# Sorted expert tiles, search steps and the end: a new division of TensorE's order in an attention and expert block

## The chip, the core and the metric

One core of a Trainium2 chip runs the whole program. The metric is the device time of one execution in microseconds (us), as the median of many; one more execution was profiled. The engines are PE (TensorE, matmuls; its weight loads are a row of their own, PEld), DVE (VectorE), ACT (ScalarE), POOL (GpSimd) and SP (SyncE, whose queue issues most DMAs). Each works through its own queue in order, and they wait for each other by semaphores.

## The reference

One block of a transformer with modulation from a condition vector, over x of 4 batches x 2048 tokens x 256 channels, all in float32:

```
mod = silu(c) @ wmod                     # six vectors per batch: sa, ca, ga, sb, cb, gb
h = layernorm(x) * (1 + ca) + sa
x = x + ga * attention(h)                # 8 heads of 32, causal softmax, a rank-one term per head
h = layernorm(x) * (1 + cb) + sb
x = x + gb * experts(h)

def experts(h):                          # h: 8192 rows of 256
    shared = sum over 2 experts of gelu(h @ up) @ down
    probs = softmax(h @ router.T)        # 16 routed experts
    top 4 of probs -> gate               # each row goes to four experts
    routed = sum over these of (gelu(h @ up_e) * gate_e) @ down_e
    return shared + routed
```

## The kernel before

The 8192 rows are cut into 16 blocks of 512; a batch has four. Block i has qb = i % 4, and its attention sees the qb + 1 blocks of its batch so far. Each block has a *search*: the largest score of every row and head is found first (`max_steps`), so that the exponentials later need no second pass. One search step (`scores`) makes the scores of 4 heads for 128 rows against up to 512 keys: 8 matmuls on PE into `ps`, then two reduces on DVE into `parts` (two more adds where the causal edge lies). Block i has 8 (qb + 1) steps. The tiles `ps` come from `mring`, three buffers of which a step needs two.

The *sums* (`sum_steps`) make the scores again, transposed (`st`), subtract the maxima by a matmul with `mT`, take exponentials on ACT (`p`), and add up values (`av`) and denominators (`dv`). Where DVE has room, two neighbouring `p` are added first (a *join*), which saves one group of `dv` matmuls.

The main loop goes over the blocks. Each turn has two parts:

- the *first part* of block i: everything that PE has to do between the sums of block i - 1 and those of block i. This is the output projection of block i - 1 (`po`), the turn and the shared expert of block i - 2 (`ptb`, `pl`, `pu_-2`, `pd_s`), projections of a coming block (`pta`, `ppq`, `ppk`, `pv`), sorted expert tiles (`px`, `pu`, `py`), and search steps of block i + 1;
- the *second part*: the sums of block i, with the search steps that are left (`rest`) put between them, and DVE's and POOL's work for other blocks (`put`).

Blocks 0 to 13 send their rows to the routed experts by sorting: in five groups (blocks 0-1, then three blocks each) the rows are scattered to DRAM by expert (`xg`, one POOL DMA for 128 rows), worked off in groups of four tiles of 128 rows (`tile_steps`: `turn` = `px`, `up` = `pu`, `down` = `py`), and gathered back with their weights (`combine_steps`: `got`, then `sum` on DVE). The first load of a group's rows (`xr`) waits for all its scatters. `fetch_ahead` issues row and weight loads two groups ahead on SP. Blocks 14 and 15 run all 16 experts densely after the loop, in pairs (`dense_steps`: `ups`, `weigh`, `routed`), with expert weights held in the keys' buffer (`resident`). This is the *end*.

The order of PE's instructions is fixed in the program by a planner with guessed costs (`T_US`, `X_US`, ..., `M_US` = 1.2 for a step on PE, `M_VE` = 2.7 on DVE). For a first part, `take_tiles` decides how many sorted tiles it gets; a loop picks m, the number of search steps; `fill_in` lays out both. It issues a step when its clock t has reached the guessed end of DVE's last step, then adds `M_US` to t and DVE's cost to that; else it takes the next piece of PE's work. When less than 3 us of pieces are left, all steps that remain come out at once. `merged` mixes two lists by their shares. `tick`, called at a pace, issues one scatter or gather.

The lines of the choice in the loop:

```
now = take_tiles(1e9 if last else max(whole - own, backlog - 105.0))
filler = own + sum(us for us, _ in now)
m, busy = 0, begin
while m < len(tops) and (
    busy + tops[m][0] <= filler + 2.0 or len(tops) - m > int(0.9 * ks)
):
```

`own` is the guessed PE time of the pieces without tiles and steps, `whole` DVE's guessed time for all steps, `backlog` that of the tiles waiting, `tops` the steps, and ks the number of summing steps of the second part.

Of the kernel before, what the change touches and what calls it, by code (L numbers as in the profile page):

```python
# [12 lines left out]
F32 = mybir.dt.float32  # L13
# [6 lines left out]
P = 128  # L20
# [74 lines left out]
def adaln_block_kernel(  # L95
# [405 lines left out]
    def tick(add=True):  # L501
        for due in sums_due:
            due[0] -= 1
        if add and sums_due and sums_due[0][0] <= 0:
            sums_due[0][1].pop(0)()
            if not sums_due[0][1]:
                sums_due.pop(0)
        if scatters:
            scatters.pop(0)()
            return  # L510
        if not gathers and ready and len(sums_due) < 2:
            gathers.extend(ready[0][0])
        if gathers:
            gathers.pop(0)()
            if not gathers:
                sums_due.append([3, ready.pop(0)[1]])


    def fill_in(pieces, tops=(), begin=0.0, pace=3.2, add=False):

        pieces, tops = list(pieces), list(tops)
        t, free, turns, next_tick = 0.0, begin, [], 1.0
        while pieces or tops:
            if t >= next_tick:
                tick(add)
                next_tick = t + pace
            if tops and (t >= free - 0.3 or sum(us for us, _ in pieces) < 3.0):
                ve, steps, turn = tops.pop(0)  # L530
                t = max(t, free)
                for s in steps:
                    s()
                t += M_US
                free = t + ve
                if turn is not None:
                    turns.append([3, turn])
                continue
# [583 lines left out]

    chain = {"steps": [], "turned": 0, "done": 0, "rows": 0, "weights": 0}

    def fetch_ahead():
        for what, n, done in (("rows", 0, "turned"), ("weights", 1, "done")):
            while chain[what] < min(len(chain["steps"]), chain[done] + 2):
                step = chain["steps"][chain[what]]  # L1130
                chain[what] += 1
                step[n](step[2])

    def tile_steps(group):
# [82 lines left out]
        for q in range(count):  # L1217
            pieces.append((U_US, lambda q=q: up(q)))
            if q + 1 < count:
                pieces += [(X_US, lambda q=q, h=h: turn(q + 1, h)) for h in range(2)]  # L1220
            pieces += [(D_US, lambda q=q, h=h: down(q, h)) for h in range(2)]
        return pieces

    def combine_steps(group):
# [56 lines left out]
    def dense_steps(i):  # L1281
# [17 lines left out]
                )  # L1299

        def up(e, u):
            if u == 0:
                acts[e] = probs.tile([P, 2, QB], F32, tag="pt", name=f"act{i}_{e}")
            pu = single([P, QB], f"pu{i}_{e}_{u}")
            products(pu, e, u)
            nc.scalar.activation(acts[e][:, u, :], pu, AF.Gelu)
# [103 lines left out]

    def take_tiles(us):
        got = []
        while tiles_to_come and us > 0:
            got.append(tiles_to_come.pop(0))
            us -= got[-1][0]
        return got

    def tiles_of(group):
        pieces = tile_steps(group)
        us, last = pieces[-1]  # L1420

        def end():
            last()
            ready.extend(combine_steps(group))

        tiles_to_come.extend(pieces[:-1] + [(us, end)])

    def free(steps):
# [4 lines left out]
    for i in range(NBLK):  # L1433
# [4 lines left out]
        if i:  # L1438
            soon, later = projected_in(i)
            outs = out_steps(i - 1, oT)  # L1440
            turns, ups, downs = [], [], []
            if i > 1:
                turns = turn_steps(i - 2)
                ups, downs = dense_steps(i - 2)
            begin = 2.5
            lead, mid = [], []
            if soon:
                new = project_steps(soon[0])
                lead = new[:2] + turns[:2] + new[2:6]
# [12 lines left out]
            mid = mid[:at] + tail  # L1462

            for n, s in enumerate(ends):
                (lead or mid).insert(2 * n + 1, (0.001, s))
            tops = [] if last else maxima(i + 1)
            state["pairs"] = not last
            own = sum(us for us, _ in lead + mid)
            whole = begin + sum(ve for ve, _, _ in tops)
            backlog = sum(us for us, _ in tiles_to_come)  # L1470
            now = take_tiles(1e9 if last else max(whole - own, backlog - 105.0))
            filler = own + sum(us for us, _ in now)
            m, busy = 0, begin
            while m < len(tops) and (
                busy + tops[m][0] <= filler + 2.0 or len(tops) - m > int(0.9 * ks)
            ):
                busy += tops[m][0]
                m += 1
            rest = tops[m:]
            left = fill_in(lead + (merged(mid, now) if now and mid else mid), tops[:m], begin)  # L1480
        if filled is not None and not scatters:
            tiles_of(filled)
            filled = None
# [103 lines left out]


    state["summing"] = True
    for e in range(0, R, 4):  # L1590
        nc.sync.dma_start(
            out=resident[:, e * 2 * C : (e + 4) * 2 * C].rearrange("p (e n) -> p e n", e=4),
# [18 lines left out]
        begin.insert(n + 1, (0.001, s))  # L1611
    begin += outs[:1] + choice[:2] + outs[1:] + ups
    begin += choice[2:-1] + downs[:1] + choice[-1:] + downs[1:]
    fill_in(begin + in_turn(pairs[:1]), pace=1.3, add=True)
    while scatters:
        tick()
    tiles_of(filled)
    choice = free(choice_steps(j, None))
    norms = second_norm_steps(j)
    late = turn_steps(j) + choice[:1] + more + choice[1:]  # L1620
    rest = take_tiles(1e9)
    amid = in_turn(pairs[1:6])
# [48 lines left out]
```

## Time and profile before

| | |
|---|---|
| median of 17 runs | 2482.15 us (2469.57 to 2492.84) |
| the profiled execution | 2475.79 us |
| its span | 2474.1 us, 42120 instructions |
| mean granted PE clock | 0.961 |
| main loop before the first sorted tile | 0 to 522.8 us |
| main loop after it (first part of block 4 to second part of block 15) | 522.8 to 2204.6 us |
| end | 2204.6 to 2474.1 us |

The parts are told apart in the timeline: a second part lasts from a block's first `st` to its last `av` or `dv`. All of the program's instructions go through one helper, so nearly all have its line (L54); they are known by the tiles they write. A timeline row has its start, its length, engine, line, operation, tiles out<-in, shapes, the number of instructions merged, and in brackets the idle time of the engine before it and what ended it. A row of busy time by stretch has the stretch, its length, then for each engine the busy time and the number of instructions, the granted clock of PE, and DMA's share and GB/s. A busy PE includes matmuls at half clock.

### The profile page before, as it was taken

The numbers are of one execution on the slowest core, as the hardware profiler recorded it, in microseconds if no ns is written. First come the engines' busy times: TensorE is split into PE (matmuls) and PEld (weight loads), VectorE is DVE, ScalarE is ACT, GpSimd is POOL, SyncE is SP. The second block draws the span as 40 slices with busy tenths as digits, with TensorE's granted clock in tenths as the row PEclk, the third lists the DMA queues.
The fourth block names the chain that finished last, engine by engine and source line by source line (L and its number), as shares of the span: only waits on it lengthen the run. The fifth ranks groups of instructions, "written<-read, shape, count | busy, mean of one in ns | idle before, by whom it ended". The sixth has DMA issues, their size and how long they took to land.

```text
span 2474.1 us, 42120 instructions
## 1 busy us (share of the span) xinstructions
PE 2328.7 (94%) x16625; PEld 1157.8 (47%) x16625; DVE 1435.3 (58%) x2789; ACT 980.3 (40%) x1391; POOL 733.5 (30%) x740
## 2 busy tenths in 40 slices
PE   7999999999999999999999998998999999998987
PEld 4443434345554334355545435354545635345754
DVE  5676565536665765646675656847665665642335
ACT  2323234543334334533343344643344345543420
POOL 3201010331101244601013352611344035464324
PEclk9889899999999899999999899999999989998998
DMA  3200401343430212322534225222656734347943
GB/s 122 90 1 10 153 10 65 126 151 112 160 120 10 70 62 97 113 93 93 188 105 154 84 63 196 79 89 88 227 175 212 247 118 157 117 147 270 341 137 112
DMA packets 219702, 306.88 MB, mean 124 GB/s; under 512 B 18544, under 2 KB 158832, under 8 KB 219504
## 3 DMA queue, kind: packets, MB, share of 16 engines
q1 hardware_dynamic: 192720, 228.89, 27.8%
q0 software_dynamic: 25536, 73.43, 9.2%
q8 instruction: 131, 2.15, 0.4%
q10 hardware_dynamic: 1248, 1.86, 0.2%
q14 instruction: 67, 0.55, 0.1%
HBM read 193.49 MB, written 114.82 MB: 125 GB/s over the span
## 4 chain that ended last, share of the span: by engine, by line
PE 83%; DVE 7%; ACT 3%; DMA 3%; issue 2%; POOL 1%; SPq 0%; POOLq 0%; ACTq 0%; DVEq 0%
PE st L54 18%; PE ps L54 13%; PE av L54 11%; PE dv L54 8%; PE pu L54 8%; PE py L54 5%; DVE parts L54 4%; PE pv L54 3%; PE po L54 2%; PE ppq L54 2%; PE px L54 2%; PE ppk L54 2%; PE pd L54 2%; PE pd_s L54 2%; PE pl L54 1%
## 5 line engine op out<-in xcount | busy, mean ns | idle before, releaser
L54 DVE TENSOR_REDUCE parts<-ps 128x2 f32<-128x1024 f32 (+3 forms) x640 | 662.4, 1063 | 366.9 <-PE ps L54 358.0
L54 ACT ACTIVATE p<-st 128x1024 f32<-128x1024 f32 (+3 forms) x640 | 539.0, 893 | 512.2 <-PE st L54 454.1
L54 PE MATMUL st<-qT,kv 32*128 32x512 f32 (+3 forms) x2560 | 406.6, 586 | 13.8 <-ACT p L54 7.4
L54 PE MATMUL ps<-kv,qT 32*128 32x512 f32 (+3 forms) x2560 | 388.4, 609 | 17.2 <-DVE parts L54 11.6
L54 POOL DMA_INDIRECT got<-yg,at x224 | 231.6, 1034 | 338.8 <-ACT p L54 102.2
L54 PE MATMUL av<-p,kv 128*32 128x512 f32 (+3 forms) x2560 | 303.4, 546 | 0.0
L74 POOL DMA_INDIRECT xg<-rows,at x219 | 219.4, 1002 | 263.0 <-ACT p L54 92.2
L54 PEld LDWEIGHTS st<-qT,kv 32*128 32x128 f32 x2560 | 144.7, 186 | 265.9 <-issue 148.4
L54 PE MATMUL dv<-p,ones 128*32 128x512 f32 (+3 forms) x2224 | 251.8, 527 | 2.7 <-DVE p L54 2.7
L54 DVE TENSOR_TENSOR ps<-ps,cmask 128x256 f32<-128x256 f32 x256 | 109.2, 427 | 200.7 <-PE ps L54 173.2
L54 PEld LDWEIGHTS ps<-kv,qT 32*128 32x128 f32 x2560 | 126.6, 192 | 205.5 <-issue 103.2
L54 POOL TENSOR_TENSOR x<-x,tmps 128x512 f32<-128x512 f32 x28 | 35.4, 1264 | 503.6 <-DVE tmps L54 503.4
L54 PE MATMUL py<-wt,tact 128*128 128x256 f32 x608 | 164.4, 406 | 6.9 <-ACT xt L54 4.8
L54 PE MATMUL st<-mT,unit 3*128 3x512 bf16 (+3 forms) x1280 | 166.7, 349 | 0.0
L54 PEld LDWEIGHTS pu<-xt,wt 128*128 128x128 f32 x1216 | 146.1, 194 | 36.4 <-issue 18.6
L54 PE MATMUL pu<-xt,wt 128*128 128x128 f32 x1216 | 157.1, 282 | 2.7 <-DMA wt<-experts 1.4
L54 ACT COPY y<-py 128x512 f32<-128x512 f32 x152 | 89.0, 585 | 166.1 <-PE py L54 166.0
L54 PEld LDWEIGHTS py<-wt,tact 128*128 128x128 f32 x608 | 112.1, 198 | 61.8 <-issue 12.9
L54 ACT COPY xt<-px 128x512 f32<-128x512 f32 x152 | 85.1, 587 | 111.1 <-PE px L54 111.1
L54 PEld LDWEIGHTS dv<-p,ones 128*32 128x32 f32 x2224 | 63.0, 110 | 138.1 <-issue 121.2
L54 DVE TENSOR_TENSOR p<-p,p 128x1024 f32<-128x1024 f32 x84 | 107.1, 1315 | 33.8 <-PE av L54 33.5
L54 ACT ACTIVATE tact<-pu 128x512 f32<-128x512 f32 x76 | 45.4, 597 | 190.5 <-PE pu L54 190.5
(290 smaller groups left out, 2476.2 us busy)
## 6 DMA issues: line engine op xcount, KB each, us to landing
wt<-experts SPq DMA_DIRECT2D x304, 256.0 KB, 4.2
xr<-xg SPq DMA_DIRECT2D x76, 512.0 KB, 4.8
yg<-y SPq DMA_DIRECT2D x76, 512.0 KB, 3.3
xg<-zeros SPq DMA_DIRECT2D x16, 1024.0 KB, 9.5
xin<-in_x SPq DMA_DIRECT2D x16, 512.0 KB, 5.7
x<-in_x SPq DMA_DIRECT2D x16, 512.0 KB, 4.5
h2d<-xnb POOLq DMA_DIRECT2D x14, 512.0 KB
pre<-x POOLq DMA_DIRECT2D x14, 512.0 KB
```

The source lines that it names most:

```text
L54: made = call(*args, **kwargs)
L74: made = call()
```

## The change

Eight edits, all in the planner, in the order of what PE, POOL and SP get; what is computed is unchanged.

1. `tick`: a gather goes ahead of waiting scatters when a set of gathers is begun, or when fewer than five sets are ready.
2. `fill_in`: the next tick comes 2.2 us later while scatters or gathers wait, otherwise after `pace`.
3. `take_tiles`: a group's second `py` is never split from what comes ahead of it.
4. Tiles for a first part: as many as fill the guessed idle time, in which a search step's PE time now counts; the backlog that may stay is 80 us instead of 105.
5. m: a step's PE time counts as cover for DVE (`+ M_US * m - 5.0`), and after a block with qb = 0 all steps go to the first part.
6. The first three pieces (one, for the last block) come ahead of any tile (`ahead`).
7. The shared activation of block 15 lies in oT's buffer.
8. The end: the last group's tiles are announced before the resident weights are loaded, with its row loads held until all scatters are out (`held`, `release`); two pairs instead of one come ahead of the tiles; block 15's turn and choice stand further ahead; the last stretch has pace 0.4 instead of 1.6.

```diff
-        if scatters:
+
+        if scatters and not (gathers or 0 < len(ready) < 5 and len(sums_due) < 2):
             scatters.pop(0)()
             return
...
             if t >= next_tick:
+                next_tick = t + (2.2 if scatters or ready else pace)
                 tick(add)
-                next_tick = t + pace
...
         for what, n, done in (("rows", 0, "turned"), ("weights", 1, "done")):
+            if what == "rows" and chain["held"]:
+                continue
...
             pieces += [(D_US, lambda q=q, h=h: down(q, h)) for h in range(2)]
+            pieces[-1][1].follows = True
...
-            if u == 0:
+            if u == 0 and i + 1 == NBLK:
+                acts[e] = once.tile([P, 2, QB], F32, tag="oT", name=f"act{i}_{e}")
+            elif u == 0:
                 acts[e] = probs.tile([P, 2, QB], F32, tag="pt", name=f"act{i}_{e}")
...
-        while tiles_to_come and us > 0:
+
+        while tiles_to_come and (us > 0 or hasattr(tiles_to_come[0][1], "follows")):
...
-            now = take_tiles(1e9 if last else max(whole - own, backlog - 105.0))
+
+
+            idle = whole - own - M_US * len(tops)
+            now = take_tiles(1e9 if last else max(idle, backlog - 80.0))
             filler = own + sum(us for us, _ in now)
             m, busy = 0, begin
+            most = 0 if qb == 0 else int(0.9 * ks)
             while m < len(tops) and (
-                busy + tops[m][0] <= filler + 2.0 or len(tops) - m > int(0.9 * ks)
+                busy + tops[m][0] <= filler + M_US * m - 5.0 or len(tops) - m > most
             ):
...
-            left = fill_in(lead + (merged(mid, now) if now and mid else mid), tops[:m], begin)
+
+            if now:
+                ahead = 1 if last else 3
+                mid = mid[:ahead] + merged(mid[ahead:], now)
+            left = fill_in(lead + mid, tops[:m], begin)
...
+    chain["held"] = True
+    tiles_of(filled)
...
-    fill_in(begin + in_turn(pairs[:1]), pace=1.3, add=True)
-    while scatters:
-        tick()
-    tiles_of(filled)
+
+    def release():
+        while scatters:
+            tick()
+        chain["held"] = False
+        fetch_ahead()
+
+    first = in_turn(pairs[:2])
+    fill_in(begin + first[:3] + [(0.001, release)] + first[3:], pace=1.3, add=True)
+    assert not scatters
     choice = free(choice_steps(j, None))
     norms = second_norm_steps(j)
-    late = turn_steps(j) + choice[:1] + more + choice[1:]
+    late = turn_steps(j) + choice[:1] + more[:1] + choice[1:3] + more[1:] + choice[3:4]
     rest = take_tiles(1e9)
-    amid = in_turn(pairs[1:6])
-    fill_in(free(norms) + merged(rest[:30], amid[:9]) + merged(rest[30:], amid[9:] + late), pace=2.4, add=True)
-    fill_in(in_turn(pairs[6:]) + much + in_turn(others), pace=1.6, add=True)
+    amid = in_turn(pairs[2:6])
+    for n, step in enumerate(choice[4:6]):
+        amid.insert(9 + 2 * n, step)
+    amid = amid[:7] + late + amid[7:]
+    fill_in(free(norms) + merged(rest, amid) + choice[6:], pace=2.4, add=True)
+    fill_in(in_turn(pairs[6:]) + much + in_turn(others), pace=0.4, add=True)
```

What the built programs' PE queues hold by part, before > after. A part of block i has search steps of block i + 1; "at its end, alone" counts the steps of a first part between which and behind which no other work stands but a projection, an output or a short turn. Parts not listed, and everything ahead of block 4, are the same.

| block | steps in first part | of these at its end, alone | steps in second part | four-tile groups (`pu`) in first part |
|---|---|---|---|---|
| 4 | 16 | 3 > 8 | 0 | 4 > 1 |
| 5 | 24 > 21 | 3 > 9 | 0 > 3 | 7 > 3 |
| 6 | 11 > 30 | 3 > 12 | 21 > 2 | 1 > 5 |
| 7 | 3 > 6 | none | 5 > 2 | 0 > 1 |
| 8 | 16 | 3 > none | 0 | 4 > 6 |
| 9 | 24 > 21 | 3 > 9 | 0 > 3 | 7 > 3 |
| 10 | 19 > 30 | 3 > 12 | 13 > 2 | 5 |
| 11 | 8 | none | 0 | 3 > 8 |
| 12 | 16 | 2 > 8 | 0 | 4 > 0 |
| 13 | 24 > 21 | 3 > 9 | 0 > 3 | 7 > 3 |
| 14 | 32 | 5 > 6 | 0 | 13 |
| 15 | 0 | none | 0 | 5 > 12 |

All `dv` matmuls together are 28 fewer after (each is two instructions of PE); no other kind changes in number.

More of the change, by code (lines that the diff above doesn't have):

```diff
@@ L1121, in place_steps @@
         return steps + [(1.4, 0, lambda: past(0)), (1.4, 0, lambda: past(1)), (0.2, 0, owners)]
-    chain = {"steps": [], "turned": 0, "done": 0, "rows": 0, "weights": 0}
+    chain = {"steps": [], "turned": 0, "done": 0, "rows": 0, "weights": 0, "held": False}
     def fetch_ahead():
         for what, n, done in (("rows", 0, "turned"), ("weights", 1, "done")):
+            if what == "rows" and chain["held"]:
+                continue
             while chain[what] < min(len(chain["steps"]), chain[done] + 2):
@@ L1424, in end @@
             ready.extend(combine_steps(group))
+        end.follows = True
         tiles_to_come.extend(pieces[:-1] + [(us, end)])
```

## The prediction, made before the changed kernel ran

> **What bounds the kernel now.** I read the page's busy times first, then busy time by stretch with the bounds of the blocks' two parts, then the timeline where TensorE (PE) and its clock lose time.
>
> ```profile
> PE 2328.7 (94%) x16625; PEld 1157.8 (47%) x16625; DVE 1435.3 (58%) x2789; ACT 980.3 (40%) x1391; POOL 733.5 (30%) x740
> PE 83%; DVE 7%; ACT 3%; DMA 3%; issue 2%; POOL 1%; SPq 0%; POOLq 0%; ACTq 0%; DVEq 0%
> 817.80:936.30 118.50, 113.77 (x894) 35.88 (x894) 81.31 (x160) 44.92 (x56) 38.44 (x41) 0.92 0.17 55
> 952.90:1058.00 105.10, 103.27 (x943) 34.11 (x942) 57.60 (x137) 60.18 (x71) 57.23 (x54) 1.00 0.36 119
> 1385.40:1482.60 97.20, 95.80 (x825) 31.90 (x825) 47.63 (x98) 44.17 (x54) 38.70 (x42) 0.94 0.23 73
> 1998.40:2071.90 73.50, 69.89 (x671) 23.41 (x670) 50.89 (x110) 44.21 (x55) 42.20 (x40) 0.98 0.39 120
> 2111.00:2204.60 93.60, 92.73 (x873) 30.52 (x873) 53.67 (x113) 59.65 (x71) 55.16 (x52) 1.00 0.29 92
> ```
>
> PE sets the end, and its total work hardly changes. A reordering can win only PE's waits and half-clock time. The stretches are the second parts of blocks 6, 7, 10, 14 and 15 (columns: length, busy PE, weight load, DVE, ACT, POOL, then granted clock, DMA share, GB/s). Blocks 6, 10 and 14 sum the same scores, yet 6, with 21 search steps inside, takes 118.5 us; 10, with 13, 97.2; 14, with none, 73.5.
>
> ```profile
> 153.40:169.60 16.20, 14.75 (x56) 5.49 (x56) 14.75 (x17) 0.72 0.00 0
> 159.34 10.30 PE L54 MATMUL ps<-kv,qT 32*128 32x512 f32 x32 [0.43 <-DVE parts L54]
> 160.72 5.37 DVE L54 TENSOR_REDUCE parts<-ps 128x2 f32<-128x512 f32 x5
> 169.57 3.78 PE L54 MATMUL po<-wo,oT 128*128 128x256 f32 x8
> 716.75 1.99 PE L54 MATMUL ps<-kv,qT 32*128 32x512 f32 x12
> 722.52 1.13 PE L54 MATMUL py<-wt,tact 128*128 128x256 f32 x4
> 1981.95:1994.30 12.35, 11.63 (x42) 4.28 (x41) 12.25 (x14) 0.58 (x1) 0.00 (x0) 0.69 0.04 14
> ```
>
> (The first row, of the search's instructions alone, lists PE, weight load and DVE, then the clock.) These are stretches in which PE's queue holds nothing but search steps ("runs"). In the first part of block 1, seven steps last from 153.49 to 169.57: 2.30 us each, set by DVE, whose two reduces take 1.2 us each. Five in block 14's take 12.35 (2.47 each); three in block 5's 5.77. One step alone costs PE some 1.0 us at full clock (1.14 busy, 1.07 to the next start). The two long runs also halve the clock (0.72, 0.69).
>
> ```profile
> 1490.48 1.09 PE L54 MATMUL px<-ident,xr 128*128 128x128 f32 x4 [7.57 <-DMA xr<-xg]
> 1729.05 6.06 POOL L54 TENSOR_TENSOR xnb<-xnb,gm 128x256 f32<-128x256 f32 x8 [13.49 <-PE py L54]
> 1735.17 0.48 PE L54 MATMUL ptb<-ident,xnb 128*128 128x128 f32 x1 [1.00 <-POOL xnb L54]
> 2244.56 1.94 PE L54 MATMUL px<-ident,xr 128*128 128x128 f32 x8 [7.83 <-DMA xr<-xg]
> 2374.87 0.62 PE L54 MATMUL pgt<-ident_b,gate 128*48 128x128 bf16 x4 [6.24 <-DVE gate L54]
> ```
>
> The largest plain waits: sorted rows that come after their scatters (block 11, and the end), the normed rows of POOL (block 13), a late gate (the end).
>
> **The change part by part.** Everything before 522.8 us stays in its order.
>
> *Runs.* The new bound on m counts a step's 1.2 us as cover for DVE, while `fill_in` still spaces steps by 1.2 us plus DVE's own 2.7. So pieces run out before steps do. In the changed order the runs at the ends of first parts 4, 5, 6, 9, 10, 12, 13, 14 are 8, 9, 12, 9, 12, 8, 9, 6 steps: 73. Before they were 3, 3, 3, 3, 3, 2, 3, 5, and 3 in block 8, which loses its run. Beyond its own 1.0 us a step of a long run costs 1.30 to 1.47; I take 1.38. After: 73 x 1.38 = 100.7. Before, seven of three steps, one of two (3.5 us by the timeline) and one of five: 7 x (5.8 - 3) + (3.5 - 2) + (12.35 - 5) = 28.4. Loss 72 (67 to 79). Behind a run stand the last projections and the next block's st on PE's queue, and ACT's exponentials wait for these.
>
> *Clock behind the runs.* After the run at 153 us the next po takes 3.78 us where the one before it took 2.00, and the first st 1.57 where the next takes 1.23: 2.1 us. After the short runs of blocks 4, 5, 9, 12, 13 the clock stays 1.00; these five now get a drop, block 8 loses one: 4 x 2.1 = 8 (0 to 11).
>
> The Trainium skill, "TensorE: Matmul & The Clock Gate", section "HAM oscillation", says PE keeps its clock unless it idles for over about 3.4 us. In the run at 153 us no idle exceeds 0.47 us, yet the clock is halved; I go by the row. By the page these 8 us would be 0.
>
> *Rows of POOL (`ahead = 3`).* In first parts 5, 9, 13 the first ptb now follows two pta; before, tile pieces came ahead of it. The xnb it needs is finished 8.3, 8.2 and 15.2 us after the second part ends (632.9 - 624.6, 1168.0 - 1159.8, 1735.1 - 1719.9). PE then has 1.1 us of work to put there (1.6 in block 13), so loses 7.2, 7.1, 13.6. Before, it lost 5.7, 6.1, 10.1 (10.8, 11.2, 15.7 us to the ptb, less 5.1, 5.1, 5.6 of work). That is 6, and half clock after the wait in blocks 5 and 9, 2 x 2.1: 10 (0 to 16). Behind that ptb waits all of the first part, so DVE's search starts later too; DVE has the slack for it there.
>
> *Second parts.* Steps leave blocks 6 (21 to 2), 10 (13 to 2), 7 (5 to 2); three each enter 5, 9, 13. A step in block 6 costs (118.5 - 73.5 - 6 dv groups at 0.95) / 21 = 1.87, 0.87 beyond its own 1.0; in block 10 0.38; in block 7 (against block 15, three dv groups, narrower steps of 0.75) 0.98. So 19 x 0.87 + 11 x 0.38 + 3 x 0.98 = 23.6, less 9 x 0.6: -18 (-4 to -20, by block 10's price or block 6's). 28 dv matmuls fewer are seven groups of 0.95: -7. Their joins (two adds of 1.3 us) fall into DVE's idle time; without that cover each would delay the dv behind it.
>
> *Scatters, gathers.* In `tick` gathers pass scatters only when few are ready. Of the 48 scatters of blocks 5 to 7, 44 now stand before block 10's second part (28 before), so block 11's row loads no longer come late: 7.6 us and 2.4 of the half clock behind it, -10 (0 to -10). The 32 gathers that leave blocks 6 and 7 for 8 and 9 cost POOL 1.03 us each, issued where it is 30% busy; block 10's first part gets 40 scatters, at 1.27 us from start to start 51 us of about a hundred.
>
> *End.* A second pair of dense experts (8.2 us) now covers the scatters, but on SP's queue the four loads of resident weights now stand ahead of the last rows load, and POOL has 18 scatters left instead of 16: -5.5 (0 to -8). The gate is chosen earlier: 6.2 and 1.7 of clock, -8. PE ends 15 us before the span; with a gather per piece (pace 0.4), 50 fit into the last ten pairs, of 48 needed: -7 (0 to -11). The sorted tiles lie denser where DMA's share is already 1.03: +2 (0 to 8). Together -18.5.
>
> At nothing: the eight expert loads that move ahead of the resident weights on SP's queue go out beside block 15's second part (DMA share 0.29); without that they would hold the rows back 4.5 us, their issue time at 2242. The last block's activation in oT's place finds oT read by po long before; else it would wait for the two po, 4 us.
>
> **Sum.** 72 + 8 + 10 - 18 - 7 - 10 - 18.5 = +36.5. The profiled execution took 2475.8 us (span 2474.1), so 2512 for it; it lies 6.4 below the median of 2482.15, so the median comes to 2519. With the terms' bounds taken as independent (15 down, 27 up), the forecast's own range is 2504 to 2546.
>
> **Rivals.**
>
> *Runs are cheap (not slower).* Place: the eight runs. The three-step runs cost 0.93 beyond their own time, since PE is a step and a half ahead of DVE when a run begins, and keep the clock. If long ones did too, runs would cost 73 x 0.93 - 28.4 = 39.5 and the clock nothing: 40.5 less, -4: 2478; without the 10 for POOL's rows 2468. It decides from 0.98 us a step downwards. For it: five short runs. Against it: two long ones at 1.30 and 1.47, and PE's lead is used up after two steps.
>
> *The end gives nothing (slower still).* If the denser tiles wait for DMA (share 1.03 at 2275 to 2300 us) and the last rows come later behind the resident weights, the 20.5 us of the end go and 6 come: 2545. For it: the saturated stretch. Against: at that share PE waited only 0.54 us for weights.
>
> *The change does not do what it says.* It speaks of keeping tiles for long searches, yet first parts 4, 5, 9, 12, 13 lose three to five groups of four sorted tiles each by the order; 6, 8, 11 and 15 gain. That speaks for the forecast.
>
> **How the numbers follow.** Forecast 0.62, cheap runs 0.22, no gain at the end 0.16. The cheap-run case lies about no change: 0.17 faster by over 0.2% (what this measurement can tell), 0.05 within it. The rest is slower: 0.78. The range goes from inside the first rival to the second: 2472 to 2548.
>
> **What would show it.** Runs of eight to twelve ps steps at the ends of the named first parts, over 2.2 us a step, with a clock near 0.7; a ptb wait of 6 us or more early in first parts 5, 9, 13; the second part of block 6 near 80 us, of block 10 near 78; no px wait in block 11; the pgt wait gone. Wrong: runs under 2 us a step, or second parts shorter than block 14's.

## The result, and the profile after

The changed kernel takes 2571.42 us (median of 8 runs, 2568.15 to 2576.84), against 2481.8 for the kernel before in the same hours (46 runs): a ratio of 1.0366, 95% interval 1.035 to 1.0382. That is some 90 us slower. The forecast was slower by 36.5, and the time lies outside its range. The profiled execution took 2568.5 us, with a span of 2566.8 (2474.1 before) and a mean granted clock of 0.937 (0.961 before).

The changed kernel's page, busy times and the chain that ended last by engine:

```profile
PE 2371.0 (92%) x16569; PEld 1187.0 (46%) x16569; DVE 1456.1 (57%) x2803; ACT 979.2 (38%) x1391; POOL 731.3 (28%) x740
PE 77%; DVE 7%; DMA 5%; issue 4%; ACT 3%; POOL 3%; SPq 0%; POOLq 0%; ACTq 0%; DVEq 0%
```

PE has 56 instructions less, as the order said, and is busy 42 us longer: nearly the same work, more of it at a lower clock. The share of the chain that is not PE's grew from 17% to 23%, with DMA, issue and POOL taking it. The loss is thus of two kinds, slower PE work and more waiting.

Busy time by stretch, changed kernel, the second parts of blocks 6, 10 and 14 (columns as in the table of before):

```profile
862.60:937.80 75.20, 74.33 (x708) 25.14 (x707) 33.98 (x85) 44.76 (x56) 25.10 (x27) 1.00 0.13 43
1423.90:1502.70 78.80, 76.54 (x699) 25.79 (x698) 29.91 (x64) 44.74 (x55) 11.67 (x14) 0.95 0.04 14
2033.40:2103.30 69.90, 69.30 (x676) 23.70 (x675) 53.02 (x119) 44.49 (x55) 42.63 (x41) 1.00 0.31 94
```

Block 6's fell from 118.5 to 75.2 us and block 10's from 97.2 to 78.8, as forecast (80 and 78). The search steps that left them went to the first parts. There, by stretch again, are block 6's first part, and within it the run of twelve steps at its end:

```profile
758.60:862.60 104.00, 97.40 (x508) 55.60 (x508) 76.62 (x94) 23.65 (x41) 5.81 (x5) 0.87 0.36 117
832.70:859.60 26.90, 25.15 (x98) 10.76 (x97) 25.95 (x30) 0.60 (x1) 0.00 (x0) 0.60 0.25 80
```

In the run DVE is busy 25.95 of 26.9 us, PE moves at DVE's pace, 2.24 us a step, and its clock is 0.60. The timeline of the changed kernel's PE shows the waits:

```profile
1774.43 0.48 PE L54 MATMUL ptb<-ident,xnb 128*128 128x128 f32 x1 [8.09 <-POOL xnb L54]
...
2109.73 1.12 PE L54 MATMUL ptb<-ident,xnb 128*128 128x128 f32 x4 [4.04 <-DVE rd L54]
...
2328.41 1.94 PE L54 MATMUL px<-ident,xr 128*128 128x128 f32 x8 [12.88 <-DMA xr<-xg]
```

The first is block 13's wait for POOL's rows, which was expected. In blocks 5 and 9, where waits of over 6 us were expected too, the first `ptb` waits only four times 1.0 to 1.4 us, 4.3 and 5.0 in all. The second row, in block 15, was not expected. The third is the end's wait for the last sorted rows: 7.83 us before, 12.88 now, where 2.3 were expected. SP's timeline, of the four loads of resident weights (`kv`) and of the last load of rows for the scatters:

```profile
2282.19 2.80 SPq L54 DMA_DIRECT2D kv<-experts  x4
2297.30 0.37 SPq L54 DMA_DIRECT2D rows<-h2d  x1
```

The rows of block 13 are loaded 13.3 us after the end began (at 2284.0); before it was 5.6. The end as a whole, by stretch up to the first `px`, then up to PE's last matmul, then the tail, first in the kernel before:

```profile
2204.60:2244.60 40.00, 27.28 (x95) 18.23 (x96) 16.88 (x46) 5.92 (x10) 25.93 (x29) 0.81 0.57 207
2244.60:2458.80 214.20, 204.29 (x954) 145.10 (x954) 75.29 (x161) 66.04 (x104) 79.54 (x84) 0.97 0.69 228
2458.80:2474.10 15.30, 0.00 (x0) 0.00 (x0) 9.51 (x20) 0.00 (x0) 6.30 (x6) 0.58 0.49 146
```

and in the changed kernel:

```profile
2284.00:2328.40 44.40, 30.20 (x120) 19.16 (x121) 15.73 (x46) 6.92 (x11) 28.07 (x29) 0.90 0.57 201
2328.40:2531.90 203.50, 197.10 (x928) 140.52 (x928) 64.60 (x132) 64.78 (x103) 64.61 (x69) 0.99 0.64 213
2531.90:2566.80 34.90, 0.00 (x0) 0.00 (x0) 19.40 (x44) 0.00 (x0) 19.89 (x20) 0.54 0.48 143
```

The middle is 10.7 us shorter: a pair of dense experts (7.6 us) moved ahead of it, and the wait for the late gate (6.2 us) went, while PE's waits for expert weights grew by 2.2. The stretch up to the first `px` took in that pair and 5.1 us more of waiting and is only 4.4 us longer: its other waits shrank and its clock rose from 0.81 to 0.90, some 8 us that the forecast didn't have. But the program goes on for 34.9 us after PE's last matmul, where it was 15.3. In that tail POOL issues 20 gathers (6 before). The changed kernel's POOL timeline shows why they are left:

```profile
2503.63 0.94 POOL L54 DMA_INDIRECT got<-yg,at  x1 [5.42 <-ACT act L54]
2504.88 0.95 POOL L54 DMA_INDIRECT got<-yg,at  x1 [0.30 <-issue]
2506.13 1.14 POOL L54 DMA_INDIRECT got<-yg,at  x1 [0.30 <-issue]
2511.25 0.95 POOL L54 DMA_INDIRECT got<-yg,at  x1 [3.98 <-ACT act L54]
2512.50 0.95 POOL L54 DMA_INDIRECT got<-yg,at  x1 [0.30 <-DVE act L54]
2518.87 0.94 POOL L54 DMA_INDIRECT got<-yg,at  x1 [5.42 <-ACT act L54]
```

Each gather takes 1.25 us from start to start. POOL gets three, then two for each pair of dense experts (7.6 us) and idles 4 to 5.4 us between. It isn't short of time: the program gives it too few gathers. The cause stands in the diff. Edit 8 asks for a pace of 0.4 us, but edit 2 replaces any pace by 2.2 us while sets of gathers are waiting, and they always are.

### The same by the terms of the forecast

For each part I worked out PE's time at full clock from the durations of its kinds of instructions (a group of four tiles 4.89 us, a full search step 1.07, a set of `dv` 0.95) and took it from the part's length. What is left is its loss. The changes of the loss, so work that only moved drops out:

| term | forecast | measured |
|---|---|---|
| first parts with runs, and block 8's, which loses its run (runs 72, clock 8, POOL's rows 10) | +90 | +82 |
| second parts (-18) and fewer `dv` (-7) | -25 | -17 |
| block 11's first part (`px` wait) | -10 | -1 |
| first parts of blocks 7 and 15 | 0 | +14 |
| everything ahead of block 4 | 0 | +2 |
| end | -18.5 | +13 |
| sum | +36.5 | +93 |

The run steps alone took 167.7 us for 73 steps (58.3 for 28 before, three of those in block 8), a loss beyond 1.0 us a step of 94.7 against 30.3: +64 of the forecast's 72.

### The profile page after: what moved, and what is told of

Its sections match the earlier page's. It is cut to its first block, busy times and chain, and to the rows that moved or that the text cites. A ratio compares the mean times of both kernels' runs of the same rounds, so it can differ in the third digit from the quotient of the medians.

```text
span 2566.8 us, 42060 instructions
## 1 busy us (share of the span) xinstructions
PE 2371.0 (92%) x16569; PEld 1187.0 (46%) x16569; DVE 1456.1 (57%) x2803; ACT 979.2 (38%) x1391; POOL 731.3 (28%) x740
## 3 DMA queue, kind: packets, MB, share of 16 engines
q1 hardware_dynamic: 192720, 228.89, 26.9%
q10 hardware_dynamic: 1248, 1.86, 0.2%
## 4 chain that ended last, share of the span: by engine, by line
PE 77%; DVE 7%; DMA 5%; issue 4%; ACT 3%; POOL 3%; SPq 0%; POOLq 0%; ACTq 0%; DVEq 0%
PE st L54 15%; PE ps L54 14%; PE av L54 10%; PE dv L54 7%; PE pu L54 6%; PE py L54 5%; DVE parts L54 3%; DMA wt<-experts 3%; PE ppq L54 2%; PE pv L54 2%; PE ppk L54 2%; PE px L54 2%; PE po L54 2%; PE pd L54 2%; PE pd_s L54 2%
## 5 line engine op out<-in xcount | busy, mean ns | idle before, releaser
L54 PE MATMUL ps<-kv,qT 32*128 32x512 f32 (+3 forms) x2560 | 437.5, 667 | 31.4 <-DVE parts L54 27.8
L54 PE MATMUL st<-qT,kv 32*128 32x512 f32 (+3 forms) x2560 | 397.9, 587 | 11.5 <-ACT p L54 8.5
L54 PEld LDWEIGHTS ps<-kv,qT 32*128 32x128 f32 x2560 | 156.6, 208 | 238.0 <-issue 96.7
L54 PEld LDWEIGHTS st<-qT,kv 32*128 32x128 f32 x2560 | 139.5, 187 | 267.7 <-issue 145.2
L54 PE MATMUL pu<-xt,wt 128*128 128x128 f32 x1216 | 163.7, 284 | 13.3 <-DMA wt<-experts 12.1
L54 PE MATMUL st<-mT,unit 3*128 3x512 bf16 (+3 forms) x1280 | 158.4, 348 | 0.0
L54 DVE TENSOR_TENSOR p<-p,p 128x1024 f32<-128x1024 f32 x98 | 119.9, 1264 | 66.6 <-PE av L54 63.1
L54 ACT COPY y<-py 128x512 f32<-128x512 f32 x152 | 88.9, 585 | 170.8 <-PE py L54 167.1
L54 POOL TENSOR_TENSOR xnb<-xnb,gm 128x256 f32<-128x256 f32 x128 | 103.7, 818 | 45.2 <-DVE xnb L54 20.6
```

Source lines behind the costliest of these rows:

```text
L54: made = call(*args, **kwargs)
```

## The experiments

One thing must be known to read them. The kernel before took 2482 to 2485 us on one chip (A here) and 2518 and 2521 on two others (B, C). So only ratios to the kernel before on the same chip are compared, and the changed kernel was run again on chip A as a measure. It was never run on B or C, and a ratio need not be quite the same on every chip: one kernel, with edit 6 undone, gave 1.0244 on C and 1.0292 on A, with intervals that don't meet. Between runs on different chips, half a percent (12 us) is therefore no difference that can be read.

| run | chip | median us | ratio to before, 95% interval |
|---|---|---|---|
| e1_pace | B | 2574.1 | 1.0219, 1.0188 to 1.025 |
| e2_loop | B | 2526.68 | 1.0043, 1.0026 to 1.0061 |
| e3_no_runs | B | 2590.0 | 1.0275, 1.0236 to 1.0314 |
| e4_both | B | 2559.94 | 1.0152, 1.011 to 1.0195 |
| c_after | A | 2573.29 | 1.0352, 1.0325 to 1.0379 |
| e5_loop_pace | A | 2459.4 | 0.9901, 0.9876 to 0.9926 |
| e6_three | A | 2464.01 | 0.9908, 0.9883 to 0.9933 |
| e8_m | A | 2548.0 | 1.0247, 1.0214 to 1.028 |
| e7_ahead | C | 2584.22 | 1.0244, 1.0219 to 1.027 |
| e9_tiles | C | 2526.22 | 1.0033, 1.0013 to 1.0052 |
| e10_spread | C | 2556.27 | 1.0128, 1.0104 to 1.0152 |
| e11_first | C | 2477.41 | 0.9828, 0.9793 to 0.9864 |
| c2_after | A | 2572.72 | 1.036, 1.0341 to 1.0379 |
| e7_again | A | 2554.68 | 1.0292, 1.0276 to 1.0308 |
| e11_again | A | 2441.12 | 0.9841, 0.9817 to 0.9865 |
| e12_order | A | 2437.6 | 0.9822, 0.9801 to 0.9843 |

### The pace at the end

```diff
-                next_tick = t + (2.2 if scatters or ready else pace)
+                next_tick = t + (2.2 if (scatters or ready) and not add else pace)
```

> The changed kernel with one line of edit 2 undone at the end only: there the next tick comes after the pace that the call asks for (0.4 us in the last stretch), not after 2.2 us. Theory: the end lost time because edit 2's 2.2 us overrides the new pace of 0.4, so that the last ten pairs issue some 3.2 gathers a pair (before: 4), and some 20 gathers at 1.25 us each are left when PE has done its last matmul. With the pace given back, PE's last matmul is followed by 15 us or less instead of 36, and the time falls by 15 to 28 us, to 2543 to 2556. Rival: the gathers wait for their rows, or POOL is short of time; then the tail stays above 30 us and the time within 6 us of 2571.

The theory held in the end's profile. Busy time by stretch in this run, PE's last 50 us and the tail:

```profile
2515.60:2565.60 50.00, 50.00 (x176) 30.77 (x174) 29.85 (x58) 6.14 (x6) 29.45 (x31) 1.00 0.40 119
2565.60:2572.30 6.70, 0.05 (x1) 0.00 (x0) 3.55 (x8) 0.00 (x0) 0.00 (x0) 0.79 0.35 117
```

POOL issues 31 gathers in the last 50 us of PE's work, and none is left for the tail of 6.7 us. The end takes 255.4 us instead of 282.8. The time itself, 2574, can't be set against 2571, since it comes from chip B, where the kernel before takes 36 us more. The same line added to the third experiment, also on chip B, took 30 us from it, a little more than the 15 to 28 expected.

### The division of the loop

```diff
-            now = take_tiles(1e9 if last else max(idle, backlog - 80.0))
+            now = take_tiles(1e9 if last else max(whole - own, backlog - 105.0))
-                busy + tops[m][0] <= filler + M_US * m - 5.0 or len(tops) - m > most
+                busy + tops[m][0] <= filler + 2.0 or len(tops) - m > int(0.9 * ks)
-                ahead = 1 if last else 3
-                mid = mid[:ahead] + merged(mid[ahead:], now)
+                mid = merged(mid, now) if mid else mid
```

> The changed kernel with edits 4, 5 and 6 undone: tiles, number of steps and order of a first part are chosen as before; the ticks, the undivided py and the end are those of the changed kernel. Theory: all that the main loop lost between 522.8 us and the end (1681.8 us before, 1759.5 after) comes from these three edits, of it some 67 from runs of search steps: the time falls by 70 to 85 us, to 2486 to 2501, and what is left above before is the end's 13 us. Rival: the other order of scatters and gathers (edits 1 and 2) bears a good part of the loop's loss; then the time stays above 2515.

The ratio is 1.0043, against 1.0352 to 1.0366 for the changed kernel: 3.1 to 3.2% or some 78 us come from edits 4, 5 and 6. These ratios are of different chips, but chip B alone says the same: the first experiment with the 30 us of the pace added back would be 2604 there, 77 more than this run. The rest, 0.4%, is the end, 282.4 us long as in the changed kernel. The order of scatters and gathers costs the loop nothing that shows.

### Runs taken apart, and both together

In the third experiment, from block 4 on, the guessed end of a step's DVE work no longer drifts with the time at which the step came out:

```diff
-                free = t + ve
+                free = (max(free, t - M_US - 4.0) if state.get('block', 0) > 3 else t) + ve
```

> The changed kernel with the spacing of search steps alone changed from block 4 on: a step's end is guessed from the end of the step before it, not from the time at which it was issued, so that no more than two steps stand together; tiles and numbers of steps are those of the changed kernel. Theory: the runs' loss is PE waiting in a run, which goes when the steps lie among other work: the eight runs take 167.7 us for 73 steps of 1.0 us of PE, so up to 94.7 and some 8 of half clock behind them come back; with steps among other work costing up to 0.38 us each (block 10's price of before), 28 of this may be given back: 2468 to 2500. Rival: DVE bounds these first parts, and the wait only moves to other places of them; then the first parts of blocks 4, 5, 6, 9, 10, 12, 13 stay within 6 us each of 72, 86, 104, 86, 106, 71 and 91 us, and the time stays above 2530.

> The edits of the last run and of the pace run together. Theory: they act in different stretches and add: 2440 to 2482, which is faster than before if both reach their middle. Rival: the gathers of the last group end with the last sorted tiles in any case, so that the sum is less than the larger one plus 5 us.

The third experiment fell far short of the theory. The changed kernel itself didn't run on chip B, but the fourth run and the first differ by this edit alone: 14 us, not 71 or more. The rival had the time right, but not its condition, since four of the seven parts became shorter by more than 6 us. The third run's profile tells why. Busy time by stretch, first part of block 6:

```profile
749.80:844.80 95.00, 89.95 (x510) 49.86 (x508) 77.36 (x94) 23.86 (x41) 5.81 (x5) 1.00 0.33 107
```

The clock is 1.00 throughout (a mean of 0.87 over 104 us before the edit, which makes 27 us at half clock), and yet the part is only 9 us shorter. The steps now come in pairs between other pieces, and a pair isn't cheap, as PE's timeline of this run shows:

```profile
763.35 2.05 PE L54 MATMUL pu<-xt,wt 128*128 128x128 f32 x16
765.33 1.99 PE L54 MATMUL ps<-kv,qT 32*128 32x512 f32 x12
767.78 1.13 PE L54 MATMUL ps<-kv,qT 32*128 32x512 f32 x4 [0.47 <-DVE parts L54]
```

Two steps take 3.5 us where they are 2.1 of work: a step needs two of `mring`'s three buffers, so the second waits for DVE's first reduce. The half clock of a run, then, is mostly no cost of its own: DVE is busy for 25.95 of the run's 26.9 us, and PE waits for it at either clock. In all, the first parts of blocks 4, 5, 6, 9, 10, 12 and 13 took 567.6 us against 615.8 in the changed kernel and 614.9 in the first experiment, which has the same loop on the same chip: 47 to 48 less. Most of it was given back: the first parts of blocks 8, 11 and 14, which had no need of the edit, became 10, 9 and 5 us longer than in the first experiment, and the second parts from block 4 on 14 us longer together.

The fourth run, with the pace on top, is 30 us faster than the third, so these two edits add. With 1.0152 it isn't faster than before, where the theory had it faster; what it lacks is what the third fell short.

A later run, on chip C, keeps the new spacing to the seven parts with long runs (`in (4, 5, 6, 9, 10, 12, 13)` in place of `> 3`):

> The third experiment's spacing in the first parts of blocks 4, 5, 6, 9, 10, 12 and 13 alone, which have the long runs; the others keep the spacing of the changed kernel. There these parts became 48 us shorter (by profiles on two chips), but the time fell by 0.8% only. Theory: the rest was given back in the first parts of blocks 8, 11 and 14, where steps that came earlier held up DVE's other work (f. i. the wait of pr for pieces); without that the ratio is 1.014 to 1.020. Rival: shortening the first parts brings waits elsewhere whatever the others do; 1.025 or more.

It gave 1.0128, near the theory's 1.014. Chip C is about as slow as B, though not the same. The seven parts take 567.9 us, blocks 8, 11 and 14 are back at 83.7, 66.9 and 123.6, and the ratio is 1.5% below the third run's. So most of the give-back came from the spacing in those three parts. By the lengths of the seven parts, about half of the runs' 95 us can be had by spacing alone.

### How many steps, or how many tiles

The number of steps in a first part is chosen as before (edit 5 undone), and then, in another run, the tiles instead (edit 4 undone):

```diff
-                busy + tops[m][0] <= filler + M_US * m - 5.0 or len(tops) - m > most
+                busy + tops[m][0] <= filler + 2.0 or len(tops) - m > int(0.9 * ks)
```

> The changed kernel with edit 5 alone undone (how many search steps a first part takes); tiles of the first parts and the end stay as changed. 52 steps move to second parts, and the runs shrink from 73 steps to 24 in runs of two to five. Theory (the runs are what costs): the runs' loss falls from 95 to some 27, the half clock behind them by some 8, and the 52 steps cost 0.38 to 0.87 us beyond their own in the second parts, 20 to 45: 31 to 56 us faster than the changed kernel, a ratio to before of 1.014 to 1.024. Rival (fewer tiles in the first parts, edit 4, is what costs, since DVE has to finish a search in a shorter part in any case): within 10 us of the changed kernel, 1.033 or more.

```diff
-            now = take_tiles(1e9 if last else max(idle, backlog - 80.0))
+            now = take_tiles(1e9 if last else max(whole - own, backlog - 105.0))
```

> The changed kernel with edit 4 alone undone: the first parts get the tiles that they had before (3 to 7 groups for the searches of 24 steps), with the changed rule for the number of steps. Long runs are left in block 6 (6 steps) and block 10 (13). Theory (a step is cheap only where other PE work of some 1.4 us lies beside it, and the tiles are that work): against before, 13 more steps in runs (18 us), 16 steps fewer in the second parts of blocks 6 and 10 (-8), the waits for POOL's rows (+10) and the end (+13) remain: a ratio to before of 1.008 to 1.018. Rival (the number of steps per part, edit 5, costs most): 1.022 or more.

With the old number of steps the runs fell to 24 steps and 50.4 us: beyond 1.0 us a step their loss is 26.4 instead of 95.6 (the changed kernel on the same chip), 69 less. The ratio fell by 1.05% only, 25 us, less than the theory's 31 to 56. By the order, 49 steps moved, not 52, and they took their cost along into the second parts. By stretch, this run's second parts of blocks 4 and 6:

```profile
585.90:623.90 38.00, 30.18 (x315) 12.47 (x314) 25.08 (x71) 13.95 (x23) 1.04 (x1) 0.95 0.01 1
...
838.40:930.40 92.00, 90.71 (x817) 30.06 (x817) 49.57 (x107) 44.16 (x55) 26.76 (x30) 1.00 0.15 50
```

They were 22.6 and 75.2 us in the changed kernel. The eight second parts that got the 49 steps are 91 us longer, 1.86 a step, of which 1.0 is its own.

With the old tiles and the new number of steps the ratio is 1.0033, no worse than with edits 4, 5 and 6 all undone (1.0043, on chip B), and below the theory's 1.008, by no more than two chips can differ. Two terms of that theory don't show in the profiles: block 11's `px` wait stays away, its first part taking 36.2 us against 43.9 in the second experiment, and the first parts of blocks 5, 9 and 13 take 309 us in all, where the second experiment without edit 6 took 312. The run of thirteen steps in block 10 is there (30.5 us): beside the second experiment its first part is 24 us longer and its second part 12 shorter, so half of it is paid back. So of the three edits the tiles (edit 4) decide: undoing them takes some 3.2% away (on another chip), the number of steps 1.05% and `ahead` 0.7%. With few tiles beside a long search, neither the old number of steps nor the spacing got the loss back alone; the two together were not run. A step costs PE 2.2 us in a run, 1.75 in a pair, 1.86 in these second parts, and little only where other work lies between one step and the next.

### What goes ahead of the tiles

```diff
-                ahead = 1 if last else 3
+                ahead = 0
```

> The changed kernel with edit 6 alone undone (no piece goes ahead of the sorted tiles of a first part by rule); runs stay about as long (66 steps). Theory: the waits of the first ptb of blocks 5, 9, 13 for POOL's rows, 4.3, 5.0 and 11.1 us in the changed kernel, are partly covered by tile pieces again, and the half clock behind them goes: 6 to 14 us faster, a ratio to before of 1.030 to 1.033. Rival: the wait moves to the next piece that needs these rows, since three groups of tiles are now spread over the whole part; then the ratio stays within 0.0015 of 1.0352.

On chip C the ratio was 1.0244, outside both theories, and might be the chip's. So it was run again, beside the changed kernel, on chip A:

> The changed kernel itself once more, as the measure for runs on a chip other than the first: on the chip of the first four experiments the kernel before took 2517.8 us, not 2481.8. Expected, if the change costs the same share on every chip: a ratio to before of 1.035 to 1.038. Rival: on the chip of the first four the loop itself has more half-clock time whatever the kernel, and the ratio falls to 1.03 or less on such a chip.

> The changed kernel, as the measure for the run after it on the same chip. If the change costs the same share on every chip, its ratio to before is 1.035 to 1.038; if half-clock time of other origin takes part of the loss, as on the chips on which before takes 2518 to 2521 us, 1.030 to 1.034.

> Edit 6 alone undone, beside the changed kernel on one chip. Theory (the wait of the first ptb for POOL's rows and the half clock behind it): by the profiles of two chips the first parts of blocks 5 and 9 are 1.5 and 7.7 us shorter, block 13's 1.5, those of 4, 7, 10 some 4 each, as they lose a step or two of their runs: 10 to 22 us less than the changed kernel. Rival: no more than 5 us, and the smaller ratio of the earlier run (1.0244) was the chip's.

The changed kernel gave 1.0352 and 1.036, so its cost holds on chip A; what it costs on B and C was not measured. Without edit 6 it is 1.0292, 18 us less, inside the 10 to 22 expected. The seven parts with runs take 594.8 us instead of 616.8. The runs bring 5 of these 22 us: they have 73 steps here too, not the 66 of the expectation, and take 163.2 us instead of 168.6. In blocks 5 and 9 three of the four short `ptb` waits of 1.0 to 1.3 us are gone, and the two parts are 10 us shorter. Block 13's 8.1 us for POOL's rows stay in both. The first part of block 15 is 81.4 us instead of 88.9, and the `ptb` that the edit had put ahead no longer waits 4.04 us for DVE's `rd`. But this part takes between 85 and 91 us in the other profiles with edit 6, and 88.9 in the run without it on chip C, so no gain is shown there.

### Old loop, new end

The second experiment's edits and the pace together leave the order of the ticks and the rebuilt end:

> The changed kernel with the division of the loop as before (edits 4, 5, 6 undone) and the pace at the end given back: what is left of the change are the order of the ticks, the undivided py and the rebuilt end. Theory: the loop then costs what it did before (in the second experiment the end began at 2248.0 us on a chip on which before is 36 us slower), and the end takes 255.4 us as in the first experiment instead of 269.5: a ratio of 0.992 to 0.997, faster than before. Rival: the shorter end of the first experiment came from sorted tiles that were already done in the loop; with before's division the tail stays and the ratio is 1.00 or more.

The ratio is 0.9901 (0.9876 to 0.9926): faster than before, by a little more than expected. The end takes 251.3 us, 18.2 less than before, so the rival falls.

In the next run three pairs, not two, come ahead of the sorted tiles:

```diff
-    first = in_turn(pairs[:2])
+    first = in_turn(pairs[:3])
-    amid = in_turn(pairs[2:6])
+    amid = in_turn(pairs[3:6])
```

> The run before with three dense pairs instead of two ahead of the sorted tiles of the end. In the first experiment the first px of the end still waits 9.29 us for its rows, with two pairs done. Theory: a third pair, some 7.6 us of PE work, lies in that wait, and PE's end comes 6 to 8 us earlier, so 0.997 of the run before. Rival: PE's end is not what ends the program: the last gathers follow the sorted tiles, which come no earlier, and one pair less is left to cover them; then the tail grows by what the wait shrinks, and the time is within 2 us of the run before.

It gained nothing (0.9908). The rival had the time right but not the reason: the tail stayed at 6.7 us. This run's timeline:

```profile
2251.96 0.35 DVE L54 TENSOR_SCALAR sum<-got,weight 128x256 f32<-128x256 f32 x1 [11.62 <-DMA got<-yg,at]
```

```profile
2259.92 5.45 PE L54 MATMUL pd<-kv,act 128*128 128x256 f32 x16 [11.88 <-DVE act L54]
```

The wait for `xr` is gone and another has its place. DVE stands 11.62 us at a `sum` whose gathers are queued on POOL behind sixteen scatters; behind it in DVE's order is the `act` that the third pair's `pd` needs.

### The first blocks, and the order of the scatters

The faster version was given the spacing of the third experiment in blocks 0 to 2 (`< 3` in place of `> 3`), whose runs are as old as the kernel before:

> The run that was faster than before (loop as before, pace at the end given back), with the spacing of the third experiment in the first parts of blocks 0 to 2, whose runs of 3, 5, 7 and 4 steps are in every kernel so far: 44.2 us for 19 steps of 1.0 us. Theory: up to 25 us of PE's waiting can be filled, but these parts hold little other work, and block 0 waits for loads; 5 to 15 us, a ratio to before of 0.984 to 0.988. Rival: DVE bounds these parts (no tiles exist yet), and nothing is gained: 0.989 to 0.992.

> The fastest kernel so far, as the measure for the run after it: a ratio to before of 0.979 to 0.987.

It gave 0.9828 on chip C and 0.9841 on chip A, 0.6% or 15 us less than without the spacing on chip A, the upper end of the theory. On chip A the first part of block 0 fell from 105.3 us to 94.3, and block 4 begins at 504.7 us instead of 525.1. Last, with edit 1 undone in this version:

```diff
-        if scatters and not (gathers or 0 < len(ready) < 5 and len(sums_due) < 2):
+        if scatters:
```

> The run before with edit 1 undone: scatters go ahead of gathers as in the kernel before. Theory: the last rows come late because two to four of block 12's scatters, and with them the load of block 13's rows, stand behind gathers and behind the loads of the resident weights; with scatters first the load of these rows is issued some 6 us after the last second part ends (5.6 before, 12.6 in the fastest kernel's loop), the last scatter ends 3 us earlier, and the wait of the end's first px falls from 10 to 7 us or less: 2 to 5 us less. Rival: gathers held back in the loop are then missing at the end, or the scatters' time is set by POOL alone: within 1.5 us, or slower.

The ratio of 0.9822 doesn't differ from 0.9841 by more than the intervals allow, but the profiles tell the two theories apart. SP's and PE's timelines of the version with edit 1, whose last second part ends at 2185.9:

```profile
2184.15 3.65 SPq L54 DMA_DIRECT2D kv<-experts  x4
2198.85 0.37 SPq L54 DMA_DIRECT2D rows<-h2d  x1
```

```profile
2229.61 0.66 PE L54 MATMUL px<-ident,xr 128*128 128x128 f32 x2 [11.20 <-DMA xr<-xg]
```

and of the version without it, where it ends at 2198.0:

```profile
2203.58 0.37 SPq L54 DMA_DIRECT2D rows<-h2d  x1
2209.32 5.30 SPq L54 DMA_DIRECT2D kv<-experts  x4
```

```profile
2238.60 1.07 PE L54 MATMUL px<-ident,xr 128*128 128x128 f32 x8 [4.03 <-DMA xr<-xg]
```

The load of block 13's rows is issued 5.6 us after that point instead of 13.0, ahead of the resident weights (`kv`) and not behind them. Its place behind them isn't what holds it up in the version with edit 1: SP has issued the weights by 2187.8 and then waits 10.8 us for block 12's scatters to land. There POOL issues the last of these 6.7 us after the last second part's end (2.9 without edit 1), and the load follows it by 6.3 us instead of 2.7. The longer landing falls together with the weights' transfers, in flight until 2200.6; whether these cause it was not tried. The `px` wait falls from 11.2 to 4.0 us and the end, in one profile of each, from 253.5 to 248.8. At 2437.6 us this version has the lowest time of all, 1.8% below before.

## Why the prediction was wrong

**Direction and main mechanism: right.** The runs stand where they were forecast, at 2.18 to 2.58 us a step. Their loss grew by 64 us (forecast 72). The second parts of blocks 6 and 10 shrank as said, block 11's `px` wait and the `pgt` wait went. The `ptb` wait of block 13 came (8.1 us and three of 1.0). Those of blocks 5 and 9 came at 4.3 and 5.0 us, not at 6 or more: the forecast let the first `ptb` wait for the last of POOL's rows (8.3 us), but each of its four transposes waits for its own rows only. The term's 10 us were met, but by luck: without edit 6 the first parts of blocks 5, 9 and 13 are 11 us shorter, while block 13's wait, the largest, stays. The rival "runs are cheap" fell. The undoing of edits 4 to 6 took some 78 us away, the share of the loop.

**The step that failed: the end, -18.5 forecast, +13.3 measured.** That is 32 of the 56 us by which the sum missed the profiled execution. In it two sentences were wrong.

"with a gather per piece (pace 0.4), 50 fit into the last ten pairs": the tail was to shrink by 7 us and grew by 19.6. Edit 2 stands in the list of the change, but the forecast didn't apply it to the call whose pace edit 8 changes. With the pace given back the tail was 6.7 us, 8.6 less than before. So the size was right for a pace that the program never had.

"A second pair of dense experts (8.2 us) now covers the scatters", a term of -5.5: the wait grew by 5.1 us. The forecast counted two more scatters and 4.5 us at most for SP's queue. In fact edit 1 let gathers pass block 12's scatters, and the load of block 13's rows had to wait for these: POOL issued the last of them 7.8 us into the end (3.0 before), and the load was issued at 13.3 instead of 5.6. With scatters first, in the version with the loop as before, the wait was 4.0. With both repaired the end takes 248.8 us, 20.7 less than before: near the forecast's 18.5.

**The rest, +25 ahead of the end.** The parts with runs came out 8 us below the forecast, the others above it. Block 15's first part (+9) was not costed. It took in seven more groups of tiles and has 4.3 us of waits for expert weights and the 4.04 for `rd`, and it varies by 3 us or more between profiles of one kernel; what edit 6 does there stays open. Block 11's wait was removed as forecast, but with the five groups of tiles that came in the part has 6.9 us of small waits for weights, pieces and buffers, where it had 1.1 beside the one removed, so the 10 us didn't show. Blocks 8, 9, 11 and 13 lost 3 to 5 us each in their second parts, where the forecast had little or nothing; what each of these came from was not tried.

**The clock behind runs** was 8 us of the sum. No run sized it. The third experiment only shows that half clock inside a run costs little, since block 6's first part went from 27 us of half clock to none and became 9 us shorter, steps moved apart included.

**"The end gives nothing", the second rival,** was nearest in time (2545). Its late rows came true (+5.1 us, where it had 6). Its saturated DMA did not: the denser sorted tiles added 2.2 us of waits for weights, as the forecast had it (2). The largest part, the tail, it didn't have, so that it came nearest is in part luck.

## What to carry to other kernels

A cheap-looking planner edit must be followed through every caller: a rate that one edit sets can be overridden by a rule that another edit adds, and what is left over comes out at the very end, where nothing hides it. Where two engines share a loop, look at what lies beside each step, not at the totals: a search step that needs 2.2 us of DVE is nearly free to PE only with other work next to it, and balancing the guessed totals left runs here in which one engine sets the pace. A wait that is covered by more work on one engine can come back through another engine's queue, so look for what stands behind the late operation there too.

## What the runs showed of the hardware

The same kernel took 2482 to 2485 us on one chip and 2518 and 2521 on two others, 1.3 to 1.6% more.

The granted clock was 0.60 in a run of twelve search steps in which PE's longest wait was 1.11 us, and 1.00 over all of the same first part when the same steps came in pairs between other matmuls, with waits of 0.47 us. The Trainium skill, "TensorE: Matmul & The Clock Gate", section "A second HAM failure mode: psum-queue depth-cycling", describes PE losing clock through frequent short idles between groups of matmuls. These rows agree with it, and not with the rule about one idle of 3.4 us that the forecast weighed. No run here shows how short or how frequent such idles may be. A run also holds nothing but matmuls of 32 rows, and no run here tells the idles from that.
